# A pairwise bilinear layer in float32: two fields per VectorE instruction also where their widths differ, and an output laid out so that all stores have one size

## The chip, the cores and the metric

The kernel runs on one core of a Trainium2 chip. The time is that of the whole program on the device, in microseconds (us). Before the change it is 1341.39 us, the median of ten runs (1341.15 to 1341.68). A profile is one execution recorded by the hardware; its engines are PE (TensorE), PEld (TensorE's weight loads), DVE (VectorE), ACT (ScalarE), POOL (GpSimd) and SP (SyncE, which here only issues DMAs).

## The reference

There are 4096 batch rows of 32 fields with 64 numbers each, and one 64 x 64 matrix for each of the 496 pairs of fields i < j. For each row and each pair, field i is multiplied by the pair's matrix, and the result element by element by field j:

```
i_idx, j_idx = np.triu_indices(32, k=1)
vi = inputs[:, i_idx, :]                       # 4096 x 496 x 64
vj = inputs[:, j_idx, :]
vdotw = jnp.einsum('bpd,pde->bpe', vi, W)
inter = vdotw * vj
return inter.reshape(B, -1)                    # 4096 x 31744, float32
```

The pairs are ordered by i, then by j. So all results of field i stand side by side in the output, (31 - i) x 64 columns wide, and the fields j that they are multiplied with stand side by side in x, too. The output is 520.09 MB; x is 33.6 MB and W some 8.1 MB.

## The kernel before

The batch is worked in 32 tiles (`t`) of 128 rows, one row per partition. Fields are taken two at a time: pair `p` of 16 holds fields 2p and 2p+1 (h = 0 and 1).

- `load_x` (L70) brings a tile of x, 128 x 2048, on ACT's DMA queue, one tile ahead, into one of two buffers.
- `transpose_x` (L75) turns x over on TensorE with an identity matrix, eight 128 x 128 blocks into two PSUM banks, and ACT copies them to `xT`. In `xT` the two fields of pair p lie above each other: field 2p on partitions 0 to 63, field 2p+1 on 64 to 127. A tile is turned over in two halves, during pairs 5 and 6 of the tile before (`PREFETCH_AT`), into one of two `xT` buffers.
- W is loaded once, before the first tile, on SP's queue: 16 DMAs (L93), one per pair, each over 128 partitions, with the matrices of field 2p on the upper 64 partitions and those of 2p+1 on the lower 64. Field 2p+1 is 64 columns narrower, and its part of the load is filled up with zeros.
- For each pair, columns are taken in chunks of 512 (`BANK`). In each chunk there is one matmul per field (L120), into one bank each of a PSUM tile of two banks; four such tiles are in use. Then VectorE multiplies the PSUM tile by x into the output ring (L130 or L139). Where both fields have the same number of columns in the chunk, one instruction does both: its operands have two runs, made by the helper `runs`. In the last chunk of a pair the widths differ by 64 (448 and 384, 320 and 256, 192 and 128, 64 and none), and there is one instruction per field.
- The output ring is an SBUF buffer of 28160 columns. A tile is stored in five pieces (`STORES`), of 7552, 6528, 5504, 6336 and 5824 columns, each by one DMA on SP's queue (L145) of 128 rows. A piece that doesn't fit behind the last one starts at the ring's beginning. In DRAM the rows of a store lie 31744 x 4 B, or 124 KiB, apart.

No order is written out beyond that of the loops. The tile framework finds from the address ranges that instructions read and write which must wait for which, and adds the semaphores. A multiply that writes a part of the ring waits so for the store that last read it, and a store waits for the multiplies that fill it. DMAs share eight semaphores in turn.

Of the kernel before, what the change touches and what calls it, by code (L numbers as in the profile page):

```python
# [1 line left out]

# [6 lines left out]

F32 = mybir.dt.float32  # L10
ALU = mybir.AluOpType

P = 128
BANK = 512

STORES = [[0, 1], [2, 3], [4, 5], [6, 7, 8], [9, 10, 11, 12, 13, 14, 15]]
PREFETCH_AT = [5, 6]
RING = 28160


@with_exitstack
def pair_bilinear_kernel(
    ctx: ExitStack,
    tc: tile.TileContext,
    x: bass.AP,
    w: bass.AP,
    out: bass.AP,
    F: int,
    D: int,
):  # L30

    nc = tc.nc
    B = x.shape[0]
    NT = B // P
    NPR = F // 2  # L50

    width = [(F - 1 - i) * D for i in range(F)]
    off = [sum(width[:i]) for i in range(F)]
    woff = [sum(width[0 : 2 * p : 2]) for p in range(NPR)]
    store_w = [sum(width[2 * p] + width[2 * p + 1] for p in g) for g in STORES]

    const = ctx.enter_context(tc.tile_pool(name="const", bufs=1))
    xpool = ctx.enter_context(tc.tile_pool(name="x", bufs=2))
    xtpool = ctx.enter_context(tc.tile_pool(name="xT", bufs=2))
    psum = ctx.enter_context(tc.tile_pool(name="ps", bufs=4, space=bass.MemoryType.PSUM))  # L60

    ident = const.tile([P, P], F32, tag="ident", name="ident")
    make_identity(nc, ident)

    def runs(tl, a, b, n):

        ap = tl[:, a : a + n]
        return bass.AP(ap.tensor, ap.offset, [list(ap.ap[0]), [b - a, 2], list(ap.ap[1])])

    def load_x(t):  # L70
        xt = xpool.tile([P, F * D], F32, tag="x", name=f"x_{t}")
        nc.scalar.dma_start(out=xt, in_=x[ts(t, P), :])
        return xt

    def transpose_x(xT, t, xt, g):  # L75

        n = 2 * BANK // P
        pt = psum.tile([P, 2 * BANK], F32, tag="ps", name=f"pt_{t}_{g}")
        for c in range(n):
            nc.tensor.transpose(pt[:, ts(c, P)], xt[:, ts(n * g + c, P)], ident)  # L80
        nc.scalar.copy(xT[:, ts(g, 2 * BANK)], pt)  # L81

    def new_xT(t):
        return xtpool.tile([P, NPR * P], F32, tag="xT", name=f"xT_{t}")

    ring = const.tile([P, RING], F32, tag="ring", name="ring")
    at = 0
    xs = {0: load_x(0)}

    w_sb = []  # L90
    for p in range(NPR):
        wp = const.tile([P, width[2 * p]], F32, tag=f"w{p}", name=f"w{p}")
        nc.sync.dma_start(out=wp, in_=w[:, woff[p] : woff[p] + width[2 * p]])  # L93
        w_sb.append(wp)

    xTs = {0: new_xT(0)}
    for g in range(2):
        transpose_x(xTs[0], 0, xs[0], g)

    for t in range(NT):  # L100
        xt, xT = xs.pop(t), xTs.pop(t)
        if t + 1 < NT:
            xs[t + 1] = load_x(t + 1)
        for s, group in enumerate(STORES):
            if at + store_w[s] > RING:
                at = 0
            osb = ring[:, at : at + store_w[s]]
            at += store_w[s]
            o0 = off[2 * group[0]]
            for p in group:  # L110
                if t + 1 < NT and p in PREFETCH_AT:
                    if t + 1 not in xTs:
                        xTs[t + 1] = new_xT(t + 1)
                    transpose_x(xTs[t + 1], t + 1, xs[t + 1], PREFETCH_AT.index(p))
                for c0 in range(0, width[2 * p], BANK):
                    pm = psum.tile([P, 2, BANK], F32, tag="ps", name=f"pm_{t}_{p}_{c0}")
                    n = [max(0, min(BANK, width[2 * p + h] - c0)) for h in range(2)]
                    for h in range(2):
                        if n[h]:
                            nc.tensor.matmul(  # L120
                                pm[:, h, : n[h]],
                                xT[h * D : (h + 1) * D, ts(p, P)],
                                w_sb[p][h * D : (h + 1) * D, c0 : c0 + n[h]],
                                start=True,
                                stop=True,
                            )
                    o = [off[2 * p + h] - o0 + c0 for h in range(2)]
                    xj = [(2 * p + h + 1) * D + c0 for h in range(2)]
                    if n[0] == n[1]:
                        nc.vector.tensor_tensor(  # L130
                            runs(osb, o[0], o[1], n[0]),
                            pm[:, :, : n[0]],
                            runs(xt, xj[0], xj[1], n[0]),
                            ALU.mult,
                        )
                    else:
                        for h in range(2):
                            if n[h]:
                                nc.vector.tensor_tensor(  # L139
                                    osb[:, o[h] : o[h] + n[h]],  # L140
                                    pm[:, h, : n[h]],
                                    xt[:, xj[h] : xj[h] + n[h]],
                                    ALU.mult,
                                )
            nc.sync.dma_start(out=out[ts(t, P), o0 : o0 + store_w[s]], in_=osb)  # L145


# [33 lines left out]
```

## Time and profile before

| | |
|---|---|
| median of ten runs | 1341.39 us |
| the profiled execution, whole | 1341.16 us |
| its span, first to last instruction | 1339.4 us |
| PE busy | 1147.9 us (86%) |
| DVE busy | 1177.6 us (88%), 1664 instructions |
| ACT busy | 66.1 us (5%) |
| DMA | 562.93 MB in 30017 packets, mean 420 GB/s |
| read from and written to HBM | 41.94 MB and 520.09 MB |
| merged multiplies (L130), 128 x 1024 | 768, 1220 ns each |
| single multiplies (L139), 64 to 448 columns | 896, 221 to 620 ns each |
| a store, from issue to landing | 21.8 to 22.8 us (medians of the five kinds) |
| the end of the chain that ended last | 54% of the span in stores, 23% in DVE, 12% in PE |

Busy times are unions; the mean durations of multiplies include what overlaps with the next one, so they add up to more. A row of busy time by stretch gives the stretch, its length, each engine's busy time and instructions, the granted TensorE clock, the DMA share and GB/s. The DMA share is the mean busy share of the core's 16 DMA engines. The DMA packet records that lie under it have a start, a duration and a size for each packet, but not the engine.

### The profile page before, as it was taken

What the parts mean: (1) busy time and instruction counts of PE and PEld (TensorE: products, weight loads), DVE (VectorE), ACT (ScalarE), POOL (GpSimd) and SP (SyncE); (2) the same over time, 40 slices, a digit from 0 to 9 for tenths busy, and PEclk for the clock granted to TensorE, in tenths of its full rate; (3) what the DMA queues carried; (4) which work ended last, traced back from release to release, by engine and by line L of the source; (5) the groups of instructions that cost most, each with busy time, mean ns of one, the idle gap of its engine ahead of it and who ended that gap; (6) DMA issues with size and microseconds to landing.
All of it is one profiled execution on the core that took longest, in us unless ns stands there. A gap on an engine that the chain in (4) does not pass through costs nothing.

```text
span 1339.4 us, 13755 instructions
## 1 busy us (share of the span) xinstructions
PE 1147.9 (86%) x5376; PEld 544.6 (41%) x5376; DVE 1177.6 (88%) x1664; ACT 66.1 (5%) x65; POOL 0.7 (0%) x6
## 2 busy tenths in 40 slices
PE   7998889888898988988888989889798897888892
PEld 3443344443444443443433434434344344444441
DVE  5999889898898988998888989989898897898993
ACT  1000000000000000000000000000000000000000
POOL 0000000000000000000000000000000000000000
PEclk9999899999998999999999999999999998999996
DMA  9999999999999999999999999999999999999996
GB/s 394 426 430 430 434 428 432 424 428 432 429 428 429 425 429 429 426 427 426 414 429 426 420 427 400 436 415 421 434 411 413 435 418 433 414 412 431 421 429 266
DMA packets 30017, 562.93 MB, mean 420 GB/s; under 512 B 3456, under 2 KB 3840, under 8 KB 5376
## 3 DMA queue, kind: packets, MB, share of 16 engines
q1 hardware_dynamic: 25344, 528.49, 92.7%
q10 hardware_dynamic: 4608, 33.56, 6.0%
q8 instruction: 42, 0.69, 0.2%
q14 instruction: 23, 0.19, 0.0%
HBM read 41.94 MB, written 520.09 MB: 420 GB/s over the span
## 4 chain that ended last, share of the span: by engine, by line
DMA 54%; DVE 23%; PE 12%; issue 9%; DVEq 0%
DMA out_dram<-ring 54%; DVE ring L130 15%; PE pm L120 9%; DVE ring L139 8%; PE pt L80 2%; DMA x<-in_x_dram 1%; DVEq L130 0%; DVEq L177 0%; DVEq L139 0%
## 5 line engine op out<-in xcount | busy, mean ns | idle before, releaser
L120 PE MATMUL pm<-w,xT 64*128 64x512 f32 (+7 forms) x4864 | 1080.8, 558 | 161.1 <-DVE ring L130 143.6
L130 DVE TENSOR_TENSOR ring<-pm,x 128x1024 f32<-128x1024 f32 x768 | 905.7, 1220 | 138.1 <-DMA out_dram<-ring 95.5
L120 PEld LDWEIGHTS pm<-w,xT 64*128 64x128 f32 x4864 | 484.3, 192 | 724.6 <-DVE ring L130 455.2
L139 DVE TENSOR_TENSOR ring<-pm,x 128x448 f32<-128x448 f32 (+6 forms) x896 | 331.8, 420 | 3.4 <-PE pm L120 2.9
L81 ACT COPY xT<-pt 128x1024 f32<-128x1024 f32 x64 | 64.8, 1013 | 1193.9 <-PE pt L80 1080.0
L80 PE MATMUL pt<-ident,x 128*128 128x128 f32 x512 | 75.8, 295 | 8.5 <-DMA x<-in_x_dram 8.5
L80 PEld LDWEIGHTS pt<-ident,x 128*128 128x128 f32 x512 | 60.3, 151 | 48.1 <-issue 37.4
L81 ACT ACT_TABLE_LOAD x1 | 1.3, 1283 | 1.7 <-PEq L173 1.7
masks.py:199 POOL TENSOR_SCALAR_AFFINE_SELECT ident<-ident 128x128 f32<-128x128 f32 x1 | 0.3, 294 | 0.1
masks.py:197 POOL MEMSET ident<- 128x128 f32 x1 | 0.2, 206 | 0.3 <-POOLq L173 0.3
L173 POOL MEMSET const-bfloat16-1.0<- 128x1 bf16 x1 | 0.1, 102 | 0.0
L173 POOL MEMSET const-uint8-127<- 128x1 uint8 x1 | 0.1, 102 | 0.0
L173 POOL MEMSET const-float32-0.0<- 128x1 f32 x1 | 0.1, 99 | 0.2 <-issue 0.2
L173 POOL MEMSET const-float32-1.0<- 128x1 f32 x1 | 0.1, 99 | 0.0
## 6 DMA issues: line engine op xcount, KB each, us to landing
out_dram<-ring SPq DMA_DIRECT2D x32, 3776.0 KB, 22.8
out_dram<-ring SPq DMA_DIRECT2D x32, 3264.0 KB, 21.8
out_dram<-ring SPq DMA_DIRECT2D x32, 3168.0 KB, 22.4
out_dram<-ring SPq DMA_DIRECT2D x32, 2912.0 KB, 22.4
out_dram<-ring SPq DMA_DIRECT2D x32, 2752.0 KB, 22.0
x<-in_x_dram ACTq DMA_DIRECT2D x32, 1024.0 KB, 14.0
w<-in_w_dram SPq DMA_DIRECT2D x1, 992.0 KB, 7.4
w<-in_w_dram SPq DMA_DIRECT2D x1, 928.0 KB, 11.7
```

Of the source, the lines that this page charges most:

```text
L80: nc.tensor.transpose(pt[:, ts(c, P)], xt[:, ts(n * g + c, P)], ident)
L81: nc.scalar.copy(xT[:, ts(g, 2 * BANK)], pt)
L120: nc.tensor.matmul(pm[:, h, : n[h]], xT[h * D : (h + 1) * D, ts(p, P)], w_sb[p][h * D : (h + 1) * D, c0 : c0 + n[h]], start=True, stop=True,)
L130: nc.vector.tensor_tensor(runs(osb, o[0], o[1], n[0]), pm[:, :, : n[0]], runs(xt, xj[0], xj[1], n[0]), ALU.mult,)
L139: nc.vector.tensor_tensor(osb[:, o[h] : o[h] + n[h]], pm[:, h, : n[h]], xt[:, xj[h] : xj[h] + n[h]], ALU.mult,)
L173: nc = bacc.Bacc("TRN2", target_bir_lowering=False, num_devices=1)
```

## The change

It has two parts.

*Multiplies.* The matmul of field 2p+1 in a pair's last chunk takes as many columns as that of field 2p, so one VectorE instruction can multiply both, with equal runs. The 64 columns more come from what lies behind the field in W: the next field's matrices, or zeros at the very end. Their products land in the output columns of the next field, where the right ones are written afterwards. x gets 64 columns more, set to zero by POOL. Where field 2p+1 has no columns in the chunk, or where a run would cross from one store to the next, there is still one instruction per field, and it is cut at the border (`multiply`). W is packed so that the fields' matrices lie side by side in each half, and loaded by ten DMAs of 64 partitions each, five groups of pairs (`LOADS`) for either half.

*Layout.* Partition q takes the 32 neighbouring batch rows 32q to 32q+31, one per tile. The host reorders x for this (tile t is x[t]). A partition's output is then one run of 32 x 31744 columns, and the result in DRAM is 128 rows of that length, 3.875 MiB each, which have the order of the reference. The ring is three slots of 10048 columns (`STORE`, 157 x 64), and a store is issued whenever one is full, wherever in a tile that is: 101 stores of 10048 columns and one of 960.

Beside these, PSUM is one tile of eight banks from which `take_banks` hands out two at a time; there is one `xT` buffer, of which the first half is rewritten for the next tile at pair 9 and the second for the current tile at pair 3.

```diff
-STORES = [[0, 1], [2, 3], [4, 5], [6, 7, 8], [9, 10, 11, 12, 13, 14, 15]]
-PREFETCH_AT = [5, 6]
-RING = 28160
+LOADS = [[0], [1], [2, 3], [4, 5, 6], [7, 8, 9, 10, 11, 12, 13, 14, 15]]
+FIRST_HALF_AT, SECOND_HALF_AT = 9, 3
+STORE = 157 * 64
+SLOTS = 3
...
-    psum = ctx.enter_context(tc.tile_pool(name="ps", bufs=4, space=bass.MemoryType.PSUM))
+    psum = ctx.enter_context(tc.tile_pool(name="ps", bufs=1, space=bass.MemoryType.PSUM))
...
+    xbuf = [const.tile([P, (F + 1) * D], F32, tag=f"x{b}", name=f"x{b}") for b in range(2)]
+    for xb in xbuf:
+        nc.gpsimd.memset(xb[:, F * D :], 0.0)
...
+    def store_to(end):
+        nonlocal stored
+        at = stored % (SLOTS * STORE)
+        nc.sync.dma_start(out=out[:, stored:end], in_=ring[:, at : at + end - stored])
+        stored = end
+
+    def in_one_store(q, n):
+        return q // STORE == (q + n - 1) // STORE
+
+    def multiply(q, pm, c, xt, xj, n):
+        while n:
+            m = min(n, STORE - q % STORE)
+            at = q % (SLOTS * STORE)
+            nc.vector.tensor_tensor(
+                ring[:, at : at + m], pm[:, c : c + m], xt[:, xj : xj + m], ALU.mult
+            )
+            q, c, xj, n = q + m, c + m, xj + m, n - m
...
-    for p in range(NPR):
-        wp = const.tile([P, width[2 * p]], F32, tag=f"w{p}", name=f"w{p}")
-        nc.sync.dma_start(out=wp, in_=w[:, woff[p] : woff[p] + width[2 * p]])
+    w_sb = const.tile([P, woff[F - 2] + width[F - 2]], F32, tag="w", name="w")
+    for g in LOADS:
+        for h in range(2):
+            a = woff[2 * g[0] + h]
+            b = woff[2 * g[-1] + h] + width[2 * g[-1] + h]
+            if h and g is LOADS[-1]:
+                b += D
+            nc.sync.dma_start(
+                out=w_sb[h * D : (h + 1) * D, a:b], in_=w[h * D : (h + 1) * D, a:b]
+            )
...
-                    if n[0] == n[1]:
-                        nc.vector.tensor_tensor(
-                            runs(osb, o[0], o[1], n[0]),
-                            pm[:, :, : n[0]],
+                q = [t * cols + off[2 * p + h] + c0 for h in range(2)]
+                xj = [(2 * p + h + 1) * D + c0 for h in range(2)]
+                if n[1] and in_one_store(q[0], n[0]) and in_one_store(q[1], n[0]):
+                    at = [v % (SLOTS * STORE) for v in q]
+                    nc.vector.tensor_tensor(
+                        runs(ring, at[0], at[1], n[0]),
+                        runs(pm, 0, BANK, n[0]),
+                        runs(xt, xj[0], xj[1], n[0]),
+                        ALU.mult,
+                    )
+                else:
+                    for h in range(2):
+                        multiply(q[h], pm, h * BANK, xt, xj[h], n[h])
+                done = q[0] + n[0] if c0 + BANK < width[2 * p] else q[1] + n[1]
+                if done // STORE * STORE > stored:
+                    store_to(done // STORE * STORE)
...
-            nc.sync.dma_start(out=out[ts(t, P), o0 : o0 + store_w[s]], in_=osb)
+    if stored < NT * cols:
+        store_to(NT * cols)
...
-    x = np.ascontiguousarray(r_inputs).reshape(B, F * D)
+    x = np.ascontiguousarray(r_inputs.reshape(P, NT, F * D).transpose(1, 0, 2))
```

## The prediction

> **What bounds the kernel now.** I read the page's slices first, then the queues, then DVE's and SP's waits, then the busy time by stretch, and last DVE's timeline at the start and the chain at the end.
>
> ```profile
> DMA  9999999999999999999999999999999999999996
> GB/s 394 426 430 430 434 428 432 424 428 432 429 428 429 425 429 429 426 427 426 414 429 426 420 427 400 436 415 421 434 411 413 435 418 433 414 412 431 421 429 266
> q1 hardware_dynamic: 25344, 528.49, 92.7%
> q10 hardware_dynamic: 4608, 33.56, 6.0%
> ```
>
> The 16 DMA engines are full in every slice but the last. Queue q1 (W and the stores) and q10 (x) take 98.7% of 16 engines' span.
>
> ```profile
> DVE ring L130 <- DMA out_dram<-ring: 95.5, 57, 3.3
> DVE ring L130 <- PE pm L120: 42.4, 47, 14.2
> SPq L145 <- DVE ring L139: 1228.4, 159, 10.5
> ```
>
> VectorE, 88% busy, is stopped by stores that have not left the ring (57 times, at most 3.3 us). SP waits only for VectorE: a store is issued when its last multiply ends. So VectorE runs ahead, ring space is the brake, and transfers set the pace.
>
> ```profile
> 1.75:27.60 25.85, 18.63 (x78) 9.99 (x78) 13.42 (x16) 3.21 (x3) 0.00 (x0) 1.00 1.02 403
> 27.60:680.00 652.40, 570.93 (x2688) 268.70 (x2688) 588.63 (x833) 32.42 (x32) 0.00 (x0) 0.96 1.00 428
> 1319.20:1327.40 8.20, 0.00 (x0) 0.00 (x0) 0.00 (x0) 0.00 (x0) 0.00 (x0) 0.65 0.97 413
> 1327.40:1338.20 10.80, 0.00 (x0) 0.00 (x0) 0.00 (x0) 0.00 (x0) 0.00 (x0) 0.50 0.06 27
> ```
>
> The columns end with clock, DMA share and GB/s. Three stages: W and two x tiles until 27.6 us, when the first packet of a store starts; stores without a gap; and 10.8 us in which the share is 0.06, one engine of 16. That engine ends at 1338.1, the others at 1327.5. In the packet records its packets are about 22 ns longer than the others' (1152 against 1119 ns at 30208 B). Five stores give an engine 40 packets per tile: 0.9 us per tile, some 28 us over 32 tiles. It sets the end.
>
> ```profile
> 14.18 3.49 DVE L130 TENSOR_TENSOR ring<-pm,x 128x1024 f32<-128x1024 f32 x3 [14.18 <-PE pm L120]
> 17.58 1.08 DVE L139 TENSOR_TENSOR ring<-pm,x 128x448 f32<-128x448 f32 x2
> 18.58 3.48 DVE L130 TENSOR_TENSOR ring<-pm,x 128x1024 f32<-128x1024 f32 x3
> ...
> 26.55 3.49 DVE L130 TENSOR_TENSOR ring<-pm,x 128x1024 f32<-128x1024 f32 x3
> ```
>
> VectorE's price: 1024 columns every 1.13 us (18.58 to 21.97 for three), 448 and 384 together 1.00.
>
> ```profile
> 1287.30 22.44 DMA out_dram<-ring
> 1309.75 0.03 issue
> 1309.77 0.05 DVEq L130
> 1309.82 0.04 issue
> 1309.87 0.13 DVE ring L130
> ```
>
> A store lands at 1309.75 and the multiply that waited for it starts 0.12 us later.
>
> [...]
>
> **The change, part by part.**
>
> *W loads.* Sixteen 128-partition loads (8.39 MB) become ten of 64 partitions (64 x 31808 x 4 B = 8.14 MB), on the same SP queue ahead of every store. At full rate W and two x tiles (2.10 MB) would take about the 25.85 us of before, and the first store would start near 28. At half rate W alone takes [...]8.14/0.2015 = 40.4 by half of the trace's 403 GB/s; with x (5 us) and the first packet at 1.75 the stores begin at 44 to 47. I take 44.5, 17 us later than 27.6. Compute does not hide this: store 0 needs pairs 0 to 2, which took VectorE from 14.18 to 26.55, so it is in SP's queue near 30, behind W. The gain side is nothing, as the bytes are the same.
>
> *Merged multiplies.* Per tile, 12 pairs of instructions become one of twice the wider one. 1024/0.96 is 1067 ns, so 1.13 us leaves 65 ns per instruction. Before: 31744/960 + 52 x 0.065 = 36.4 us a tile (timeline: 36.4). After: 1458 instructions over 32466 columns a tile: 33.8 + 3.0 = 36.8. As the 64 extra columns are overwritten later, the built program also has 360 multiplies that wait for the one before: 11 a tile, 0.1 to 0.2 us each, 1 to 2 us. With 1 us of waits for PE, VectorE needs 39 to 40 us a tile; the transfers need 40.9 ((1338.1 - 27.6)/32). Covered, but barely: without this cover each us a tile costs 32. TensorE's extra columns, two memsets on POOL and the single xT buffer (halves rewritten at pairs 9 and 3, after pairs 0 to 7 and 8 to 15 have used them) lie beside that too.
>
> *Stores.* 160 become 101 of 10048 columns and one of 960. The page's 30017 packets become some 20,160: 616 fewer per engine[...], -2 us. Packets of 40192 B extrapolate to 1486 ns, the same rate.
>
> *Row pitch.* A partition now writes 3.875 MiB (31 x 128 KiB) from its neighbour. [...]I take nothing[...].
>
> *A new wait.* Fields 2p and 2p+1 go into one instruction with two runs in the ring. When the first run lies at the end of slot 2 and the second at the start of slot 0, the step is negative (29632, then -29440), and the range spanned holds all of slot 1. In the built program these multiplies wait for the store of slot 1, the one issued just before. This happens for 15 of the stores: 5, 8, 20, 29, 35, 47, 50, 53, 56, 65, 68, 74, 80, 89 and 95. The store that must follow cannot be issued before the wait ends, so all 16 engines run dry. Queued behind the multiply are all later multiplies; SP's store waits for them, and PE after four more chunks.
>
> Price of a drain: last packet to landing 0.45 us (packet and landing records); landing to multiply 0.12; the multiplies up to the end of the store; SP 0.02; issue to first packet 1.0 with idle engines (first W load: 0.74 to 1.75), 2.2 to 4 with busy ones (x loads); I take 1.4. The fixed part is 1.99 x 15 = 30 us. The multiplies are 30 instructions of 23,680 columns; at 3.49 us per 3072 columns, 27. Together 57. Bounds: 45 (short latency, x packets filling part) to 80. Elsewhere the wait is for the slot's own old store, two stores back; one store is then still queued (12 us) and only a few multiplies (under 4 us) stand before the next issue, so nothing is lost. After a drain both other slots are free and VectorE refills each in about 12.5 us while each transfer takes 12.3 plus the drain; it stays ahead.
>
> **Sum against the profiled execution.** Stores from 44.5; 1310.5 us of transfers as before (1338.1 - 27.6); -2; +57; +1.3 to the end of the span: 1411.3. The execution lies 1.8 above its span (1341.16 against 1339.4), and the median 0.2 above that: 1413 us, 5% slower.
>
> **Rivals.**
> 1. *The drains are hidden*: the range test does not bite, or the store before has long landed. 1413 - 57 = 1356. For it: VectorE and the transfers are nearly equal in pace. Against it: VectorE was held by the ring 57 times.
> 2. *The pitch costs write bandwidth*:[...]
> 3. *The slow engine goes* (faster): its 28 to 30 us vanish with the new rows, giving 1413 - 57 - 30 = 1326 when there are no drains. It decides only if drains and W together stay under 32 us, so below 1 us per drain beside a W of 17; the latencies alone are 1.6. With the drains it is 1383. Its packets ran at 865 ns like the others' when alone at the end, so the excess may depend on where it writes.
> 4. *W loads at full rate*: 1413 - 16.5 = 1396, inside the forecast's range.
>
> **How the numbers follow.** Forecast with its bounds (1383 to 1435) 0.72; rival 2 0.14; rival 1 0.09; rival 3 without drains 0.03; 0.02 is left for no change. The range 1380 to 1450 takes in the forecast, its bounds and the lighter half of rival 2, and leaves out rival 1. A change under 0.2% cannot be told from none here: faster 0.03, same 0.02, slower 0.95.
>
> **What would show it.** W: first store packet near 44, the 64-partition loads near 200 GB/s. Drains: DVE waits for stores of several us, about 15 of them with the DMA share falling, and lower digits in the DMA row. Covered multiplies: DVE near 37 us busy a tile. Pitch: GB/s between the drains below 428. Slow engine: one-engine tail again. I am wrong if the DMA row stays at 9 throughout, or if DVE waits for PE take the place of its waits for stores.

## The result and the profile after

The changed kernel takes 1424.09 us (median of 8 runs, 1422.11 to 1425.2); the kernel before took 1341.31 us in the runs beside it (29 runs, 1340.72 to 1341.69). The ratio is 1.0617, with a 95% interval of 1.0607 to 1.0626: 6.2% slower, where 1413 us had been predicted. The span of the profiled execution is 1423.7 us.

First the page of the changed kernel, with the slices and the queues:

```profile
DMA  9999999989998989999899899998989899989899
GB/s 226 361 434 380 386 425 422 426 373 405 427 426 354 424 354 407 424 431 430 343 375 407 375 422 436 413 389 357 426 367 424 356 390 442 423 369 410 357 421 389
q1 hardware_dynamic: 15488, 528.24, 88.3%
q10 hardware_dynamic: 4608, 33.56, 6.2%
```

The DMA row, all nines before but for the last slice, has eights scattered over its whole length, and the GB/s under them are 343 to 375. q1's packets fill a smaller share of a longer span than before (88.3% against 92.7%), for the same bytes. And the first two slices have lost most: 226 and 361 GB/s, where they had 394 and 426.

Next VectorE's waits:

```profile
DVE ring L174 <- DMA out_dram<-ring: 115.9, 16, 12.9
DVE ring L174 <- PE pring L163: 38.7, 28, 16.7
```

Before, VectorE waited 57 times for a store, at most 3.3 us. Now the merged multiplies wait 16 times and up to 12.9 us: few and long waits in place of many short ones. 15 of the 16 fall at the multiplies that cross the ring's end.

The busy time by stretch shows the stages. The columns are stretch, length, busy time (and instructions) of PE, PEld, DVE, ACT and POOL, granted clock, DMA share and GB/s:

```profile
1.75:46.30 44.55, 31.59 (x114) 15.38 (x114) 24.02 (x25) 3.19 (x3) 0.00 (x0) 0.92 1.01 230
170.00:298.00 128.00, 117.39 (x553) 51.26 (x554) 124.26 (x152) 7.09 (x7) 0.00 (x0) 1.00 1.01 430
512.00:518.10 6.10, 0.00 (x0) 0.00 (x0) 0.00 (x0) 0.00 (x0) 0.00 (x0) 0.62 0.57 244
518.10:523.10 5.00, 3.21 (x8) 1.48 (x10) 4.49 (x5) 0.00 (x0) 0.00 (x0) 0.50 0.09 40
523.10:535.10 12.00, 11.43 (x52) 4.98 (x49) 11.32 (x15) 0.00 (x0) 0.00 (x0) 0.97 1.01 432
548.90:551.10 2.20, 1.68 (x10) 0.47 (x10) 2.10 (x3) 0.00 (x0) 0.00 (x0) 1.00 0.86 220
```

W and x take until 46.3 us, where the first store starts (before: 27.6): the DMA share is full but the rate is 230 GB/s. Where no drain falls, as from 170 to 298 us, stores and x run at 430 GB/s, like before. Around 518 us is one drain (the queue of transfers running empty): the DMA engines run out one after the other (at 515.5 us 14 of the 16 have a packet, at 516.0 five, at 517.5 one; share 0.57 over 6.1 us), then for 5 us almost nothing moves, then it is full again. The last row is for later: a short time without a store packet, in which the engines are busy with x.

The same drain in the order of time:

```profile
518.61 3.49 DVE L174 TENSOR_TENSOR ring<-pring,x 128x1024 f32<-128x1024 f32 x3 [10.96 <-DMA out_dram<-ring]
...
522.01 0.22 DVE L130 TENSOR_TENSOR ring<-pring,x 128x64 f32<-128x64 f32 x1
...
522.26 24.85 SPq L119 DMA_DIRECT2D out_dram<-ring  x3
```

Store 34's last packet ends at 518.1. The multiply that had waited 10.96 us starts at 518.61, four multiplies finish store 35, SP issues it at 522.26, and its first packet starts at 523.1. Over the whole run the packet records have 15 such gaps between store packets, 1.9 to 5.0 us long, 50.0 us together; in three of them some x packets move. Another 19 us without a store packet lie between the stores that follow a drain, but these are hardly a loss. Of the 14 that are longer than 0.4 us, 12 have a DMA share of 0.83 or more, as in the row from 548.90: x is on the engines, and it has to be moved at some time anyway. In the other two, 0.9 and 1.5 us long, nothing moves. From the first store to the last packet no engine has a packet for 44.2 us in all, and times in which only a part of the engines has one add up to some 32.5 us of all 16.

### The profile page after: what moved, and what is told of

Read it like the earlier page. It is cut to its first block, busy times and chain, and to the rows that moved or that the text cites. A ratio compares the mean times of both kernels' runs of the same rounds, so it can differ in the third digit from the quotient of the medians.

```text
span 1423.7 us, 13143 instructions
## 1 busy us (share of the span) xinstructions
PE 1181.3 (83%) x5376; PEld 531.6 (37%) x5376; DVE 1213.3 (85%) x1458; ACT 66.1 (5%) x65; POOL 0.9 (0%) x8
## 3 DMA queue, kind: packets, MB, share of 16 engines
q1 hardware_dynamic: 15488, 528.24, 88.3%
## 5 line engine op out<-in xcount | busy, mean ns | idle before, releaser
L163 PE MATMUL pring<-w,xT 64*128 64x512 f32 (+4 forms) x4864 | 1111.8, 568 | 193.1 <-DVE ring L174 171.1
L174 DVE TENSOR_TENSOR ring<-pring,x 128x1024 f32<-128x1024 f32 (+3 forms) x1062 | 1100.9, 1081 | 184.6 <-DMA out_dram<-ring 115.9
L163 PEld LDWEIGHTS pring<-w,xT 64*128 64x128 f32 x4864 | 474.5, 193 | 810.1 <-DVE ring L174 613.2
L130 DVE TENSOR_TENSOR ring<-pring,x 128x64 f32<-128x64 f32 (+7 forms) x396 | 138.8, 394 | 10.4 <-PE pring L163 2.8
L110 ACT COPY xT<-pring 128x1024 f32<-128x1024 f32 x64 | 64.9, 1013 | 1314.4 <-PE pring L109 1240.7
L109 PE MATMUL pring<-ident,x 128*128 128x128 f32 x512 | 72.9, 287 | 31.7 <-DVE ring L174 23.0
L109 PEld LDWEIGHTS pring<-ident,x 128*128 128x128 f32 x512 | 57.1, 145 | 64.3 <-DVE ring L174 53.0
## 6 DMA issues: line engine op xcount, KB each, us to landing
w<-in_w_dram SPq DMA_DIRECT2D x1, 1296.0 KB, 27.6
```

The costliest lines, as they stand in the source:

```text
L130: nc.vector.tensor_tensor(ring[:, at : at + m], pm[:, c : c + m], xt[:, xj : xj + m], ALU.mult)
L163: nc.tensor.matmul(pm[:, h * BANK : h * BANK + n[0]], xT[h * D : (h + 1) * D, ts(p, P)], w_sb[h * D : (h + 1) * D, a : a + n[0]], start=Tr ...
L174: nc.vector.tensor_tensor(runs(ring, at[0], at[1], n[0]), runs(pm, 0, BANK, n[0]), runs(xt, xj[0], xj[1], n[0]), ALU.mult,)
```

## The experiments

Each kernel ran beside the kernel before, whose median was 1341.2 to 1341.3 us in all of them.

**Both costs taken out, one at a time and together.** In the first kernel, W is loaded over all 128 partitions:

```diff
     for g in LOADS:
-        for h in range(2):
-            a = woff[2 * g[0] + h]
-            b = woff[2 * g[-1] + h] + width[2 * g[-1] + h]
...
-            nc.sync.dma_start(
-                out=w_sb[h * D : (h + 1) * D, a:b], in_=w[h * D : (h + 1) * D, a:b]
-            )
+        a = woff[2 * g[0]]
+        b = woff[2 * g[-1]] + width[2 * g[-1]]
+        nc.sync.dma_start(out=w_sb[:, a:b], in_=w[:, a:b])
```

> Only the W loads are changed: five DMAs over all 128 partitions in place of ten over 64. Theory ([...]nothing hides the load): the first store packet starts near 28 us in place of 46.3 and the time falls by 17 to 19 us, to about 1406. Rival (the drained engines later make up for a late start, so W is not on the path): the first store starts early as well, but the time stays at 1424.

It took 1406.26 us, 17.8 less than the changed kernel, and its first store started at 28.3:

```profile
1.75:28.30 26.55, 17.82 (x74) 8.58 (x76) 13.64 (x15) 3.21 (x3) 0.00 (x0) 1.00 0.95 394
```

394 GB/s here, 230 in the changed kernel. A packet of 16128 B, a size that both have, takes 606 ns here and 1256 ns there. The rival falls: the drains do not absorb a late start.

In the second, a multiply whose two runs lie in different laps of the ring becomes two:

```diff
+    def in_one_lap(q):
+        return q[0] // (SLOTS * STORE) == q[1] // (SLOTS * STORE)
...
-                if n[1] and in_one_store(q[0], n[0]) and in_one_store(q[1], n[0]):
+                if n[1] and in_one_store(q[0], n[0]) and in_one_store(q[1], n[0]) and in_one_lap(q):
```

> Only the multiplies are changed whose two runs lie in different laps of the ring: they become one instruction per field. Theory (the wait for the store issued just before drains the engines 15 times, 50 us, and the slow restart after it costs another 19 us): about 1355, a DMA share of 9 tenths throughout. Rival 1 (VectorE and TensorE are too slow for the transfers anyway, and the wait only shows it): above 1385, with DVE waiting for PE in place of stores. Rival 2 (the one slow DMA engine of before is only reset by the drains and comes back without them): 1365 to 1375 with a tail in which one engine works.

It took 1356.91 us, 67.2 less than the changed kernel. Its page and VectorE's waits:

```profile
DMA  9999999999999999999999999999999999999997
DVE ring L133 <- DMA out_dram<-ring: 25.4, 29, 2.2
DVE ring L177 <- DMA out_dram<-ring: 22.1, 15, 2.6
DVE ring L177 <- PE pring L166: 34.5, 26, 17.2
```

The nines are back, and no wait for a store is longer than 2.6 us. 33 more instructions are all that differs on VectorE, so it was the waits that cost, not the engine's pace. How the cost divides is not as the text above has it: its 19 us of "slow restart" are the gaps in which x moved. From the first store to the last packet this kernel needs 68.9 us less (1307.2 against 1376.1). 44.2 of them are the time in which no engine had a packet, which is gone here. 19.3 are times with a part of the engines (13.3 here, 7.5 of it in the last 15 us, against 32.5). The other 5.4 are packets that take a little less time here.

The third has both edits:

> Both repairs together, W over 128 partitions and no multiply across the ring's end. Theory (the two costs are separate and add): 1424 - 18 - 69 = 1337, just below the kernel before. Rival (slow engine comes back): 1347 to 1356.

1338.74 us (14 runs), a ratio to the kernel before of 0.9981 (0.9973 to 0.9989). The two savings add: 17.8 + 67.2 = 85.0, measured 85.35. This version is faster than both kernels, by 0.2% against the kernel before.

**Half of the drains.** The multiply across the ring's end stays one instruction in even laps:

```diff
     def in_one_lap(q):
-        return q[0] // (SLOTS * STORE) == q[1] // (SLOTS * STORE)
+        lap = [v // (SLOTS * STORE) for v in q]
+        return lap[0] == lap[1] or lap[0] % 2 == 0
```

> The changed kernel with half of the drains: a multiply across the ring's end stays one instruction in even laps of the ring and becomes two in odd ones, which leaves 7 waits for the store just issued (before stores 8, 20, 50, 56, 68, 74 and 80) of 15. Theory (each drain costs what the mean of the 15 did, 67.2/15 = 4.5 us): 1356.9 + 7 x 4.5 = 1388. Rival (the next drain soon takes back what a removed one gave, or the gain of the repair came from other shapes): at least 1405, or near 1357.

It took 1384.86 us: seven drains cost 28.0 us, 4.0 each, where the mean of the 15 was 4.5. The cost goes with the number of drains.

**The W loads on the kernel before.** The other way round, the kernel before with its W loads cut in halves:

```diff
-        nc.sync.dma_start(out=wp, in_=w[:, woff[p] : woff[p] + width[2 * p]])
+        for h in range(2):
+            nc.sync.dma_start(
+                out=wp[h * D : (h + 1) * D, :],
+                in_=w[h * D : (h + 1) * D, woff[p] : woff[p] + width[2 * p]],
+            )
```

> The kernel before, with each of its 16 W loads cut into two of 64 partitions, and nothing else. Theory ([...]half the rate, not hidden): the stores start 18 us later and the time rises to 1359. Rival (it was the order or size of the five groups of pairs in the changed kernel that cost): 1341 to 1345.

It took 1359.82 us, 18.6 more than the kernel before beside it. Its first stretch, in the columns of above:

```profile
1.75:45.00 43.25, 35.28 (x156) 17.79 (x156) 28.71 (x36) 5.21 (x5) 0.00 (x0) 0.96 0.99 242
```

A full DMA share at 242 GB/s, where the kernel before had 403, with 16 pairs of loads instead of five groups: the number of partitions decides, not how W is grouped. The packets are as large as before and take nearly twice as long (7424 B: 544 ns against 281).

**The row layout alone.** The kernel before with 32 neighbouring batch rows per partition, everything else left:

```diff
-        nc.scalar.dma_start(out=xt, in_=x[ts(t, P), :])
+        nc.scalar.dma_start(out=xt, in_=x[t])
...
-            nc.sync.dma_start(out=out[ts(t, P), o0 : o0 + store_w[s]], in_=osb)
+            nc.sync.dma_start(out=out[:, t * cols + o0 : t * cols + o0 + store_w[s]], in_=osb)
```

> The kernel before with the row layout alone (each partition holds 32 neighbouring batch rows; the same five stores per tile, multiplies and W loads). Theory (the slow DMA engine depends on the addresses it writes in DRAM, and the layout removes it): about 1322, no tail of one engine. Rival 1 (it depends on the size or number of the stores, or on the drains): 1341, the tail stays. Rival 2 (a pitch of 3.875 MiB costs write bandwidth): above 1345, with less than 428 GB/s in full stretches.

1341.32 us, a ratio of 1.0 (0.9991 to 1.0008). My theory fell and the first rival held:

```profile
27.60:680.00 652.40, 575.13 (x2688) 275.15 (x2688) 587.90 (x832) 32.38 (x32) 0.00 (x0) 0.95 1.00 428
...
1327.40:1338.20 10.80, 0.00 (x0) 0.00 (x0) 0.00 (x0) 0.00 (x0) 0.00 (x0) 0.50 0.06 27
```

The rate is 428 GB/s as before, so the pitch of 3.875 MiB costs nothing, and the last 10.8 us still belong to one engine, so other addresses in DRAM do not take its lag away. In the changed kernel this tail is missing. There each drain waits for the engine that is last, so the lag is probably paid in small parts; the records do not name the engine, so that it is the same one each time is not shown. The twice repaired kernel, without drains, has the tail again:

```profile
1316.00:1325.70 9.70, 0.00 (x0) 0.00 (x0) 0.00 (x0) 0.00 (x0) 0.00 (x0) 0.50 0.98 423
1325.70:1334.00 8.30, 0.00 (x0) 0.00 (x0) 0.00 (x0) 0.00 (x0) 0.00 (x0) 0.50 0.16 65
```

**Merging alone.** The twice repaired kernel with one multiply per field again where the widths differ (`n[1] == n[0]` in place of `n[1]` in the condition; the matmuls stay as wide):

> The twice repaired kernel (W over 128 partitions, no multiply across the ring's end) with one multiply per field again where the widths differ; the matmuls stay as wide. Theory (VectorE lies beside the transfers either way): the time stays within 2 us of 1338.7 while the number of multiplies rises from 1491 to 1840. Rival (VectorE is so near the transfers' pace that 350 more instructions cost): 1342 or more.

1341.04 us (13 runs; ratio to the kernel before 0.9998, 0.999 to 1.0006), 2.3 more than with merging. That is just outside what the theory allowed and below what the rival asked for. VectorE's waits:

```profile
DVE ring L133 <- DMA out_dram<-ring: 55.7, 36, 3.3
DVE ring L172 <- DMA out_dram<-ring: 39.8, 20, 3.5
DVE ring L172 <- PE pring L161: 29.0, 22, 13.9
```

And in the merged version, the twice repaired kernel:

```profile
DVE ring L133 <- DMA out_dram<-ring: 22.5, 25, 2.1
DVE ring L172 <- DMA out_dram<-ring: 22.3, 16, 2.7
DVE ring L172 <- PE pring L161: 20.2, 10, 13.7
```

VectorE waits 95.5 us for stores without merging, against 44.8 with it: with more instructions it is not later, it waits more. So the 2.3 us are lost in the transfers, not on VectorE, and why is open.

**Smaller stores.** The twice repaired kernel with `STORE = 157 * 32` and `SLOTS = 6`:

> The twice repaired kernel with stores of half the size, six slots of 5024 columns in the same ring: 203 stores of 20 KB rows. Theory ([...]the slow engine's excess goes with its bytes): 816 more packets per engine cost 3 to 4 us: 1342. Rival (the slow engine loses 22 ns in each packet, whatever its size): 18 us more, 1357, or part of it.

1353.22 us, 14.5 more: between the two, nearer the rival. The end of its span:

```profile
1335.00:1349.00 14.00, 0.00 (x0) 0.00 (x0) 0.00 (x0) 0.00 (x0) 0.00 (x0) 0.50 0.06 26
```

One engine works alone for 14 us, where it was 8 with stores of twice the size. From the first store on, the packet time rose by only 5.3 us an engine (1304.6 against 1299.3), 6.6 ns for each of the 808 more store packets, so most of the 14.5 is time in which engines had no packet. Counted for all 16, such time is 12.4 us with 808 large store packets per engine (the twice repaired kernel), 20.0 with 1280 (the kernel before) and 25.6 with 1616 (this one): 15 to 16 ns for each packet, whatever its size. So in these three kernels the lag goes with the number of packets and not with the bytes, as the rival had it, at a somewhat smaller rate than its 22 ns.

## Why the prediction was right

The direction, the size and the two causes were right; the sum was 11 us too low. It came that near partly by luck: in the price of a drain one part was too high and another was left out. Term by term, as the prediction put them:

- *W loads, 17 us.* Right: the first store started at 46.3 us (predicted 44 to 47), and the load cost 17.8 us in the changed kernel, 18.6 in the kernel before. The half rate was an assumption: the kernel before has no load of 64 partitions. Half of its 403 GB/s gives the 47, and the 44 was an estimate of mine. The runs show it: in the larger loads over 64 partitions a packet moves 12.8 bytes per ns, which is 205 GB/s for 16 engines (230 over the whole stretch, with x), where packets of W over 128 partitions move 26.6 (16128 B in 606 ns). Why 64 partitions have half the rate is not shown. That nothing hides it was right, too: store 0 was issued at 34.4 us, behind W, 12 us before its first packet.
- *The drains, 57 us.* The mechanism and the number, 15, were right. The parts that were priced measure nearly as estimated: from the last packet to the multiply 0.56 us in the median (0.57), the multiplies 28.4 us in all (27), from issue to the first packet 0.83 us in each drain (1.4). As x packets move in some of them, only 44.2 us without any packet are left over the whole run, 13 less than the 57. But the repair gave back 67.2.
- *The step that was sized wrong* is where the price of a drain begins: at the last packet. It took all 16 engines as busy up to there. They are not, as the multiply waits for the store's last engine: of store 34 the 16 landing records run from 515.51 to 518.42 us, the multiply starts at 518.61, and the share before that is 0.57 over 6.1 us. Against the kernel without drains this running out comes to 19.3 us, and longer packets to another 5.4; the prediction had nothing for either. So a drain costs 4.5 us, not 3.8: about 2.9 with no packet, 1.3 with a part of the engines, 0.4 in longer packets. This division is a count from the packet records of one execution of each kernel; the runs show the sum, 67.2, and that seven drains cost 28.0.
- *"It stays ahead"* held nearly. Stores after a drain did start late, but x filled the engines' time; 2.4 us of the 44.2 were lost there. VectorE's waits for PE, without the first one at the start, are 22.0 us, against 17.3 in the kernel without drains that has the same W loads (34.5 - 17.2). In the drain at 518 the granted clock is 0.50, in the gap at 548.90 it is 1.00; whether the clock has any part in the cost was not tested.
- *Covered multiplies.* VectorE is busy 1213.3 us, 37.9 a tile; predicted near 37, and 1 to 2 more for dependent multiplies. In the trace 335 multiplies start 0.10 us after the end of the one before, where most others start 0.08 to 0.09 us before it: 0.18 us each, if these are the dependent ones (360 in the built program). (The 0.96 columns per ns of that sum follow from the single multiplies of the kernel before: 221 ns for 64 columns, 620 for 448.) The cover held where there were no drains: removing them alone gave back 67.2 us. That merging would change nothing was nearly right, it brings 2.3 us.
- *Fewer packets, -2 us.* The 2 us were an estimate of mine without a measured time per packet behind it; the smaller stores showed 6.6 ns for each packet more. The packets of 40192 B took 1486 ns, as extrapolated. The twice repaired kernel ends 2.6 us below the kernel before, with this and the merging as its gains. Without the merging nothing is left (1341.04), so the fewer packets are not shown to bring anything by themselves.
- *Row pitch, 0.* Right, but an estimate of mine, as before has no row of this pitch. Stores whose rows lie 3.875 MiB apart run at 428 GB/s with the row layout alone and at 430 in the changed kernel, where rows 124 KiB apart ran at 428. No other pitch was run, so nothing here bounds what one could cost.
- *The slow engine* was taken as unchanged. The tail that I had expected to see again is not there, as every drain already waits for the last engine. The 22 ns per packet were badly supported: the two times beside them, 1152 and 1119 ns, are 33 apart, and in the tail the engine's packets take as long as others (865 ns at 23296 B). Rival 3, in which the lag goes with the new rows, fell with the row layout alone.

Rivals 1, 2 and 4 fell as well: the drains cost 67.2 us, the rate between them is 430 GB/s, and the stretch of the W loads ran at 230 GB/s, where W over 128 partitions had 394 and 403.

From the profiled spans: the first store is 18.7 us later, and from there to the last packet it takes 65.6 us more than before (1376.1 against 1310.5). Of these, 44.2 are without any packet, 12.5 with a part of the engines (32.5 against 20.0, as the kernel before has its lag, too), and 8.8 are longer packets. Together that is the 84.3 us between 1339.4 and 1423.7.

## What to carry to other kernels

In the programs built here, an access pattern with two runs counts for the dependence test as the whole range between them; when the second run lies before the first in a ring, that range holds the slots in the middle, and the instruction waits for a store that it doesn't touch, here up to 12.9 us. In a kernel that lives on always having a transfer queued, one such wait for the youngest store empties the queue (4.5 us each here): look in the built program for what each wait names, and count how many stores are still behind it. Price such a drain from the moment when the first engine has nothing left, not from the last packet: about 1.3 of the 4.5 us were times with a part of the engines. And a load before the loop is part of the transfer time when transfers set the pace, so its partitions matter as well as its bytes: W in loads of 64 partitions in place of 128 cost 17.8 us in the changed kernel and 18.6 in the kernel before.

## What was not expected of the hardware

One DMA engine of the 16 ends some 7 to 14 us after the others in every version without drains. Moving all rows in DRAM changed nothing about it (10.8 us with both layouts); halving the packets' size made it worse (14 us against 8), and over three kernels the time that is lost goes with the number of store packets, some 16 ns for each. The cause is open. The records hold a lead that no run tested: in the twice repaired kernel 43 of the 47 store packets that took over 0.1 us longer than usual, with no x beside them, ran at the same time as a packet of the queues q8 and q14, which bring instructions. Whether these fall on the late engine the records do not say, and the number of instruction packets is much the same in the three kernels, while the lag is not.
